# Attention in steps of four key tiles instead of two, in a two-layer convolution and attention kernel

## The chip, the cores and the metric

The kernel runs on one core of a Trainium2 chip. The metric is the device time of one execution in microseconds, taken as the median of several runs. TensorE (PE) does the matrix products, VectorE (DVE) and ScalarE (ACT) empty its results from PSUM and do the elementwise work, GpSimd (POOL) does further elementwise work, and SyncE (SP) issues the loads and stores. All data are 32-bit floats; a 512-column product in that type is two instructions on TensorE.

## The reference

The input x has 8 images of 512 channels, 32 x 32 positions each. Two layers follow one another, each added to its own input.

```python
# layer 0
t = cbs(gn(x), cv1_w)                  # 1x1, 512 -> 512; cbs = convolution, batch norm, SiLU
ys = [t[:, :256], t[:, 256:]]
for i in range(2):
    z = cbs(ys[-1], m_cv1_w[i], pad=1)  # 3x3, 256 -> 256
    q, k, v = qkv(z)                    # 1x1, 256 -> 768; 4 heads of 64
    a = softmax(q^T (k + rw + rh) / 8)  # 1024 queries x 1024 keys per head
    ys.append(ys[-1] + silu(bn(m_cv2[i] @ (a v))))
x = x + cbs(concat(ys), cv2_w)          # 1x1, 1024 -> 512
# layer 1
x = x + conv1x1(gn(x), w_eff)[:, perm]  # w_eff masked and scaled by tables made from S and T
```

gn is a group norm over 32 groups without weights; batch norm uses fixed statistics.

## The kernel before

**Units.** The 8 images with 2 attention blocks each are 16 *slots* (`slots`, two images in turn, block 0 of both, then block 1 of both). A slot is four *units*: a pair of heads (hp) times a half of the 512 queries. A unit has eight key tiles (`KT`) of 128 keys; a tile's logits are 128 keys x 2 heads x 512 queries and take two PSUM banks. `units` holds all 64 in order.

**A unit's life** (class `Unit`). `logits(t)` forms a tile on TensorE (`lg`, L510), copies it to a tile `st` on ScalarE (L517), and from tile 1 on takes the running maximum over keys on VectorE (`mx`, L522). `top` (L530, L531) transposes the maximum and reduces it; `spread` (L539) broadcasts its negative into PSUM (`mb`). `soften(t)` (L544, VectorE) adds `mb` to the tile, `exponent(t)` (L548, ScalarE) takes the exponential in place, and POOL adds the tile to the running sum in four quarters (L555). `values(t)` (L562, TensorE) multiplies by v into one bank, `po`. `finish` (L576, L579) sums the running sum over the keys with a product by ones (`den`) and copies it to `rb`; `divide` (L583, L585, VectorE) takes the reciprocal of one half of the queries and multiplies `po` by it into q.

**The order.** The main loop runs unit u's softmax and values, and next to them the logits of the following unit `nxt`. It does so in steps of two key tiles: the last two tiles' values of the unit `before`, or two tiles' values of u, then two tiles' logits of `nxt`. Between them `advance(share)` emits *filler*, the other layers' products, from `slot_filler`: the first convolution (`conv1`, L248), the 3x3 convolution of the next slot (`conv3`, six products in a row transform, L313), the query, key and value projections (`project`), `conv_m2`, `conv2` and the last layer (`last`), most of them through `accumulate` (L175). The slot is cut into 4 x 10 nominal steps, and filler is emitted up to a given share of the slot's total at steps 0.7, 1.4, 2, 4, 6, 8 and 10 of each unit. Chains of order-only dependencies (`in_turn` for VectorE, `act_turn` for ScalarE, `pe_turn` for TensorE) fix the order of the attention's instructions among themselves, and of some of the transform's, on each engine. `Clock` issues some filler work (norms, transforms) when its estimated due time is reached.

**Buffers.** PSUM has eight banks: five in turn (`ps_f`) for logits, filler, `mt` and `den`; two for `mb`; one for `po`. In SBUF the pool `stp` holds 10 tiles of logits (4 KB a partition), `wp` four weight tiles, `wt` three temporaries of the convolution's transform, `kvp` three tiles each of keys (tag k) and values. Small parameters (`bn_sb`, `s_sb`, `rw_sb`, `rh_sb`, L86 to L89, and `tri`, L681) have their own places. The parameters are used while the kernel starts, last by `positions(1)`, which adds `rw` and `rh` on POOL. All loads and stores after the start go through `load` (L77, L78) on SP's queue, in order.

**The end.** After the last unit `finish`, the last two tiles' values and `divide` follow, then filler that was held back: `conv_m2`, `conv2` and `last` of the last image.

Of the kernel before, what the change touches and what calls it, by code (L numbers as in the profile page):

```python
# [15 lines left out]
F32 = mybir.dt.float32  # L16
AF = mybir.ActivationFunctionType
ALU = mybir.AluOpType
# [4 lines left out]
P = 128  # L23
NB = 8
CT = 4
IT = 2
F = 32
HW = F * F
HALF = 512
NBLK = 2  # L30
HD = 64
NG = 16
KT = 8
NGR = 17

BN_CV1, BN_CV2, BN_M1, BN_M2, BN_ALL = 0, 4, 8, 12, 16
# [3 lines left out]
def conv_preact_kernel(ctx: ExitStack, tc: tile.TileContext, x, cv1, cv2, mcv1, qkv, mcv2, bn, rw, rh, conv, s_in, t_in, out):  # L40
    nc = tc.nc
    stt = nc.vector.scalar_tensor_tensor

    def pool(name, bufs, **kw):
        return ctx.enter_context(tc.tile_pool(name=name, bufs=bufs, **kw))

    const = pool("const", 1)
    dram = pool("dram", 1, space=bass.MemoryType.DRAM)
    small = pool("small", 2)
    qp = pool("qp", 2)  # L50
    kp_ = pool("kvp", 3)
    stp = pool("stp", 10)
    one = pool("one", 1)
    wp = pool("wp", 4)
    gx = pool("gx", 4)
    wm = pool("wm", 1)
    gy = pool("gy", 4)
    gr = pool("gr", 2)
    tp = pool("tp", 3)
    wt = pool("wt", 3)  # L60
    ps_m = pool("ps_m", 1, space=PSUM)
    ps_o = pool("ps_o", 1, space=PSUM)
    ps_f = pool("ps_f", 5, space=PSUM)
# [1 line left out]
    def pair(p, tag, name):  # L65
        return p.tile([P, 2, HALF], F32, tag=tag, name=name)

    def bank(name):
        return ps_f.tile([P, HALF], F32, tag="bank", name=name)
# [4 lines left out]
    def flat(t):  # L74
        return t.rearrange("p a b -> p (a b)")
# [7 lines left out]
        return t  # L83


    bn_sb = const.tile([P, 4, BN_ALL], F32, name="bn_sb")  # L86
    s_sb = const.tile([P, 2, CT, NG], F32, name="s_sb")
    rw_sb = const.tile([P, NBLK, IT, F], F32, name="rw_sb")
    rh_sb = const.tile([P, NBLK, IT, F], F32, name="rh_sb")  # L89


    w_m1 = [[dram.tile([P, IT, IT, 3, P], F32, name=f"w_m1_{i}_{r}") for r in range(6)] for i in range(NBLK)]
# [89 lines left out]
    def in_turn(instruction):  # L182

        if turn:
            tc.add_manual_dep(instruction.ins, turn.pop().ins.name, IN_ORDER, reason="order of VectorE")
        turn.append(instruction)

    def act_turn(instruction):

        if act_last:  # L190
            tc.add_manual_dep(instruction.ins, act_last.pop().ins.name, IN_ORDER, reason="order of ScalarE")
        act_last.append(instruction)
# [300 lines left out]
    class Unit:  # L493
# [52 lines left out]
        def exponent(self, t):  # L546
            st = flat(self.st[t])
            act_turn(nc.scalar.activation(st, st, AF.Exp))  # L548
            if t == 1:
                self.acc = pair(one, "acc", f"sum_{self.name}")  # L550
            for j in range(4 if t else 0):

                part = slice(256 * j, 256 * j + 256)
                so_far = self.st[0] if t == 1 else self.acc
                nc.gpsimd.tensor_tensor(flat(self.acc)[:, part], flat(so_far)[:, part], st[:, part], ALU.add)  # L555
# [81 lines left out]
    def tables():  # L637

        scr = flat(pair(gr, "gr", "scr")).rearrange("p (a k g) -> p a k g", a=8, g=NG)
        gi = scr[:, 0]  # L640
        gi_i = scr[:, 7].bitcast(mybir.dt.int32)
        nc.gpsimd.iota(gi_i, pattern=[[0, 2 * CT], [1, NG]], base=-NG, channel_multiplier=0)
        nc.vector.tensor_copy(gi, gi_i)
        full = [P, 2 * CT, NG]

        sc = s_sb.rearrange("p a k g -> p (a k) g")
        cols = small.tile([P, 4, 2 * CT], F32, tag="cols", bufs=1, name="cols")
        top, rsum, gain, idx = (cols[:, j] for j in range(4))

        def wide(v):  # L650
            return v.unsqueeze(2).to_broadcast(full)

        e, oh, lower = scr[:, 1], scr[:, 2], scr[:, 3]
        nc.vector.tensor_reduce(top, sc, AX.X, ALU.max)
        nc.vector.tensor_tensor(e, sc, wide(top), ALU.subtract)
        nc.scalar.activation(e, e, AF.Exp)
        nc.vector.tensor_reduce(rsum, e, AX.X, ALU.add)
        nc.vector.reciprocal(rsum, rsum)
        nc.vector.tensor_tensor(e, e, wide(rsum), ALU.mult)
        nc.vector.tensor_reduce(gain, e, AX.X, ALU.max)  # L660

        nc.vector.tensor_tensor(oh, e, wide(gain), ALU.is_equal)
        nc.vector.tensor_tensor(oh, oh, gi, ALU.mult)
        nc.vector.tensor_reduce(idx, oh, AX.X, ALU.min)
        nc.vector.tensor_tensor(oh, gi, wide(idx), ALU.is_equal)
        nc.vector.tensor_tensor(lower, gi, wide(idx), ALU.is_gt)


        pre = scr[:, 4]
        nc.vector.tensor_reduce(pre[:, 0], lower[:, CT:].rearrange("p c g -> p g c"), AX.X, ALU.add)  # L670
        for k in range(1, CT):
            nc.vector.tensor_tensor(pre[:, k], pre[:, k - 1], oh[:, CT + k - 1], ALU.add)
        yield
        oht = pair(gr, "gr", "oht")[:NG]
        for a in range(2):
            ps = bank(f"oht_{a}")
            for k in range(CT):
                nc.tensor.transpose(ps[:NG, ts(k, P)], oh[:, CT * a + k], ident)
            nc.vector.tensor_copy(oht[:, a], ps[:NG])

        tri = small.tile([P, P], F32, tag="tri", bufs=1, name="tri")  # L681
        nc.gpsimd.affine_select(
            out=tri, in_=ones, pattern=[[1, P]], compare_op=ALU.is_gt, fill=0.0, base=0, channel_multiplier=-1
        )
        rank = small.tile([P, CT], F32, tag="rank", bufs=1, name="rank")
        ps = bank("rank").rearrange("p (k g) -> p k g", g=NG)[:, :CT]
        nc.tensor.matmul(ps, ones, pre[:, :CT], start=True, stop=False)
        nc.tensor.matmul(ps, tri, oh[:, CT:], start=False, stop=True)
        nc.vector.tensor_tensor(e[:, :CT], ps, oh[:, CT:], ALU.mult)
        nc.vector.tensor_reduce(rank, e[:, :CT], AX.X, ALU.add)  # L690
        table_results.extend((gain, oht, rank))
        yield
# [48 lines left out]
    units = [Unit(im, i, hp, half) for im, i in slots for hp in range(IT) for half in range(2)]  # L741
# [25 lines left out]
    clock = Clock()  # L767
# [216 lines left out]
    first, second = images[:2]  # L984
# [8 lines left out]
    clock.at(11.0, lambda: start_norm(second, tiles2))  # L993
    clock.at(12.0, lambda: transform_weights(0))
    ranks = tables()
    clock.at(14.0, lambda: next(ranks))
    clock.at(26.0, lambda: next(ranks))
# [26 lines left out]
    before = None  # L1024
    for s in range(len(slots)):
        needed, total, todo = slot_filler(s)
        state = {"done": 0.0}

        def filler():
            for us, g in todo:  # L1030
                start = state["done"]
                for cost in g:
                    clock.tick(cost)
                    state["done"] += cost
                    yield

                state["done"] = max(state["done"], start + us)

        fill = filler()

        def advance(share):
            goal = max(share * total, min(1.0, share / 0.74) * needed + 0.1)
            while state["done"] < goal:
                if next(fill, "end") == "end":
                    break

        steps = 4 * (KT + 2)
        for j in range(4):
            u = units[4 * s + j]
            nxt = units[4 * s + j + 1] if 4 * s + j + 1 < len(units) else None  # L1050
            base = j * (KT + 2)

            advance((base + 0.7) / steps)
            u.top()
            clock.tick(0.9)
            advance((base + 1.4) / steps)
            u.spread()
            clock.tick(0.9)
            advance((base + 2) / steps)
            for t in range(0, KT, 2):  # L1060
                if before and t == 0:
                    before.finish()
                    clock.tick(0.9)
                u.soften(t)
                u.soften(t + 1)
                if t:
                    u.exponent(t)

                lag = u if t else before
                if lag:  # L1070
                    lag.values((t - 2) % KT)
                    lag.values((t - 1) % KT)
                    clock.tick(2.0)
                if before and t == 0:
                    before.divide(0)
                    before.divide(1)
                if nxt:
                    nxt.logits(t)
                    nxt.logits(t + 1)
                    clock.tick(2.0)  # L1080

                if not t:
                    u.exponent(t)
                u.exponent(t + 1)
                advance((base + 4 + t) / steps)
            before = u
        for _ in fill:
            pass

    before.finish()  # L1090
    before.values(KT - 2)
    before.values(KT - 1)
    before.divide(0)
    before.divide(1)
    im = images[NB - 1]
# [55 lines left out]
```

## Time and profile before

| quantity | value |
|---|---|
| median of 3 runs | 3161.52 us (3156.13 to 3167.02) |
| profiled execution, own time | 3162.82 us |
| its span | 3161.1 us |
| granted TensorE clock, mean | 0.996 |
| busy: TensorE, VectorE, ScalarE, POOL | 3077.0, 2049.9, 1721.0, 1398.4 us |
| logits (L510), values (L562) on TensorE | 510.9, 497.8 us in 2048 instructions each |
| softens (L544), VectorE | 512 of 1215 ns |
| maxima (L522), VectorE | 896 of 0.68 us |
| reciprocals (L583), VectorE | 128 of 1723 ns |
| copies of logits (L517), ScalarE | 1024 of 597 ns |
| exponents (L548), ScalarE | 512 of 1068 ns |
| table loads, ScalarE | 1283 ns each |
| sums (L555), POOL | 1792 of 0.77 us |

The busy time of an engine is the time in which an instruction of its own was running; the span less the busy time is idle. In the waits an entry names the engine and the operation that waited, what it waited for, and then the time in total, the number of times and the longest. In a timeline an entry has the start, the length, the engine, the source line, the operation, output and inputs, and how many like instructions are put together; the idle time ahead of it and its releaser may stand in brackets. The profile gives busy time on TensorE with modelled ends, so that neighbouring blocks overlap a little; their starts are measured.

### The profile page before, as it was taken

How to read it: one execution, taken by the hardware profiler on the slowest of the kernel's cores; microseconds unless marked ns; L12 is line 12 of the kernel's file. 1: busy time of each engine (PE TensorE's matmuls, PEld its weight loads, DVE VectorE, ACT ScalarE, POOL GpSimd, SP SyncE). 2: the span in 40 equal slices, each digit the busy share in tenths (PEclk: the TensorE clock that was granted, in tenths of full speed). 3: DMA queues.
4: the chain of work that ended last, by engine and by line, in shares of the span. 5: the costliest groups of instructions: out<-in, count | busy, mean ns of one | idle time of the engine just before them, and what ended most of it. 6: DMA issues, size and time to landing. Idle time of an engine off the chain costs nothing.

```text
span 3161.1 us, 34185 instructions
## 1 busy us (share of the span) xinstructions
PE 3077.0 (97%) x11668; PEld 1515.3 (48%) x11668; DVE 2049.9 (65%) x2718; ACT 1721.0 (54%) x2349; POOL 1398.4 (44%) x1867
## 2 busy tenths in 40 slices
PE   7999999998999999999999999999999999999999
PEld 3645354454445454455445454454445454453333
DVE  5446577567667576667666676767666676767642
ACT  3245765855655555644656455544656455546621
POOL 2104444546444554455444454445444464444520
PEclk9999999999999999999999999999999999999999
DMA  8852352421233232424233332424233332413356
GB/s 289 292 182 74 130 180 87 153 77 63 88 116 131 79 128 71 149 84 148 84 116 130 114 127 70 153 85 136 91 110 130 120 120 70 150 64 120 120 205 217
DMA packets 142014, 399.35 MB, mean 126 GB/s; under 512 B 13072, under 2 KB 14352, under 8 KB 141840
## 3 DMA queue, kind: packets, MB, share of 16 engines
q1 hardware_dynamic: 141120, 396.94, 36.6%
q8 instruction: 92, 1.51, 0.2%
q14 instruction: 82, 0.67, 0.1%
q10 hardware_dynamic: 720, 0.23, 0.0%
HBM read 317.42 MB, written 79.69 MB: 126 GB/s over the span
## 4 chain that ended last, share of the span: by engine, by line
PE 75%; DVE 4%; ACT 4%; issue 2%; DMA 1%; POOL 1%; SPq 0%; ACTq 0%; DVEq 0%; POOLq 0%
PE cv L175 15%; PE m L313 13%; PE po L562 12%; PE lg L510 12%; PE l L175 7%; PE qk L175 6%; PE v L405 3%; PE m L175 3%; PE den L576 2%; PE mb L539 2%; PE mt L530 1%; ACT st L517 1%; DVE st L544 1%; ACT st L548 1%; DVE mx L522 1%
## 5 line engine op out<-in xcount | busy, mean ns | idle before, releaser
L555 POOL TENSOR_TENSOR sum<-sum,st 128x256 f32<-128x256 f32 x1536 | 1132.0, 771 | 552.1 <-ACT st L548 547.7
L522 DVE TENSOR_TENSOR mx<-mx,lg 128x512 f32<-128x512 f32 x768 | 477.8, 682 | 417.6 <-ACT st L517 417.4
L517 ACT COPY st<-lg 128x512 f32<-128x512 f32 x1024 | 525.0, 597 | 356.1 <-PE lg L510 331.7
L548 ACT ACTIVATE st<-st 128x1024 f32<-128x1024 f32 x512 | 539.1, 1068 | 304.1 <-DVE st L544 302.9
L544 DVE TENSOR_TENSOR st<-st,mb 128x1024 f32<-128x1024 f32 x512 | 604.4, 1215 | 60.2 <-PE mb L539 60.2
L555 POOL TENSOR_TENSOR sum<-st,st 128x256 f32<-128x256 f32 x256 | 185.1, 754 | 788.8 <-ACT st L548 788.8
L313 PE MATMUL m<-plane,w_m 128*128 128x256 f32 x2304 | 528.8, 383 | 4.9 <-ACT cv2s L130 2.7
L562 PE MATMUL po<-st,v 128*64 128x512 f32 x2048 | 497.8, 605 | 18.2 <-ACT st L548 16.2
L510 PE MATMUL lg<-q,k 64*128 64x512 f32 x2048 | 510.9, 617 | 2.9 <-ACT y L130 2.9
L313 PEld LDWEIGHTS m<-plane,w_m 128*128 128x128 f32 x2304 | 426.4, 189 | 129.5 <-issue 45.1
L175 PE MATMUL cv<-y,w_cv 128*128 128x512 f32 x1024 | 464.5, 599 | 7.9 <-ACT cv2s L130 4.6
L510 PEld LDWEIGHTS lg<-q,k 64*128 64x128 f32 x2048 | 177.3, 186 | 328.2 <-issue 267.4
L175 PEld LDWEIGHTS cv<-y,w_cv 128*128 128x128 f32 x1024 | 185.8, 190 | 248.1 <-issue 226.4
L562 PEld LDWEIGHTS po<-st,v 128*64 128x64 f32 x2048 | 128.8, 136 | 323.6 <-issue 237.3
L175 PE MATMUL cv<-x,w_cv 128*128 128x512 f32 x512 | 237.0, 610 | 10.6 <-ACT y L130 3.7
L175 PE MATMUL l<-x,w_l 128*128 128x512 f32 x512 | 236.9, 606 | 7.9 <-DVE mx L522 6.9
L175 PE MATMUL qk<-z,w_qkv 128*128 128x512 f32 x512 | 234.0, 600 | 1.4 <-DVE mx L522 1.4
L583 DVE RECIPROCAL rb<-rb 128x256 f32<-128x256 f32 x128 | 215.5, 1723 | 26.0 <-ACT rb L579 25.8
L531 DVE TENSOR_REDUCE nm<-mt 128x4 f32<-128x512 f32 x128 | 82.3, 684 | 144.7 <-PE mt L530 144.7
L579 ACT COPY rb<-den 128x512 f32<-128x512 f32 x64 | 37.3, 583 | 230.4 <-PE den L576 230.4
L175 PEld LDWEIGHTS cv<-x,w_cv 128*128 128x128 f32 x512 | 95.3, 194 | 132.0 <-issue 109.3
L175 PEld LDWEIGHTS l<-x,w_l 128*128 128x128 f32 x512 | 93.4, 191 | 130.4 <-issue 112.2
(145 smaller groups left out, 2408.8 us busy)
## 6 DMA issues: line engine op xcount, KB each, us to landing
w_m<-w_m SPq DMA_DIRECT2D x96, 768.0 KB, 4.8
w_cv<-in_cv SPq DMA_DIRECT2D x90, 512.0 KB, 3.5
y<-y SPq DMA_DIRECT2D x64, 512.0 KB, 4.8
x<-in_x SPq DMA_DIRECT2D x56, 512.0 KB, 5.2
y<-y SPq DMA_DIRECT2D x64, 256.0 KB, 3.5
k<-r SPq DMA_DIRECT2D x32, 512.0 KB, 3.6
res<-y SPq DMA_DIRECT2D x32, 512.0 KB, 4.0
xr<-in_x SPq DMA_DIRECT2D x32, 512.0 KB, 4.1
```

Of the source, the lines that this page charges most:

```text
L175: nc.tensor.matmul(ps, w, moving, start=(n == 0), stop=(n == len(terms) - 1))
L313: nc.tensor.matmul(ps[:, ts(co, 256)].rearrange("p (t x) -> p t x", x=F), w[:, co, c, dx], u[:, 9 * c : 9 * c + 8, dx : dx + F], start=(j ...
L405: nc.tensor.matmul(ps[:, ts(j, P)], z[:, c, ts(4 * j4 + j, P)], w[:, c, 512 + P * hp : 512 + P * hp + P], start=(c == 0), stop=(c == IT - 1),)
L510: nc.tensor.matmul(lg[h], self.k[r, ts(t, P)], self.q[r, self.hp, ts(self.half, HALF)], start=True, stop=True)
L517: act_turn(nc.scalar.copy(st[:, h], lg[h]))
L522: in_turn(nc.vector.tensor_tensor(self.mx[:, h], so_far[:, h], lg[h], ALU.max))
L531: nc.vector.tensor_reduce(self.nm[:, h], mt, AX.X, ALU.max, negate=True)
L544: in_turn(nc.vector.tensor_tensor(st, st, flat(self.mb), ALU.add))
L548: act_turn(nc.scalar.activation(st, st, AF.Exp))
L555: nc.gpsimd.tensor_tensor(flat(self.acc)[:, part], flat(so_far)[:, part], st[:, part], ALU.add)
L562: nc.tensor.matmul(self.po[HD * h : HD * h + HD], self.v[:, t, ts(h, HD)], self.st[t][:, h], start=(t == 0), stop=(t == KT - 1),)
L583: nc.vector.reciprocal(self.rb[:, r], self.rb[:, r])
```

## The change

The main loop takes steps of four key tiles: values of two, logits of two, values of two, logits of two, with no filler between them. The values now lag four tiles instead of two. The softens and exponents of the third and fourth tile of a step are issued after the step's logits, one soften and one exponent in turn; `divide` follows both values and both logits blocks. The filler is emitted at steps 0.5, 2, 6 and 9.3 of each unit (`top` now stands ahead of the first). The ring of logits grows from 10 to 12 tiles. To make room, the weights have three tiles instead of four, the transform's temporaries two instead of three, and the small parameters lie in one tile of the keys' ring. The last unit's running sum is made on VectorE, one addition of a whole tile each (seven), in the fixed order of that engine, instead of in 28 quarters on POOL; and four tiles' values follow its denominator at the end.

```diff
-    stp = pool("stp", 10)
+    stp = pool("stp", 12)
-    wp = pool("wp", 4)
+    wp = pool("wp", 3)
-    wt = pool("wt", 3)
+    wt = pool("wt", 2)
...
-    bn_sb = const.tile([P, 4, BN_ALL], F32, name="bn_sb")
-    s_sb = const.tile([P, 2, CT, NG], F32, name="s_sb")
-    rw_sb = const.tile([P, NBLK, IT, F], F32, name="rw_sb")
-    rh_sb = const.tile([P, NBLK, IT, F], F32, name="rh_sb")
+    par = kp_.tile([P, HW], F32, tag="k", name="par")
+    def param(first, shape):
+        return par[:, first : first + P].rearrange("p (a b c) -> p a b c", b=shape[0], c=shape[1])
+    s_sb = param(0, (CT, NG))
+    rw_sb = param(128, (IT, F))
+    rh_sb = param(256, (IT, F))
+    bn_sb = par[:, 512 : 512 + 4 * BN_ALL].rearrange("p (a b) -> p a b", b=BN_ALL)
...
             if t == 1:
                 self.acc = pair(one, "acc", f"sum_{self.name}")
+            if t and self is units[-1]:
+                so_far = self.st[0] if t == 1 else self.acc
+                in_turn(nc.vector.tensor_tensor(flat(self.acc), flat(so_far), st, ALU.add))
+                return
...
-        tri = small.tile([P, P], F32, tag="tri", bufs=1, name="tri")
+        tri = par[:, 384:512]
...
-            advance((base + 0.7) / steps)
             u.top()
             clock.tick(0.9)
-            advance((base + 1.4) / steps)
+            advance((base + 0.5) / steps)
             u.spread()
             clock.tick(0.9)
             advance((base + 2) / steps)
-            for t in range(0, KT, 2):
+            half = KT // 2
+            for t in range(0, KT, half):
...
                 lag = u if t else before
-                if lag:
-                    lag.values((t - 2) % KT)
-                    lag.values((t - 1) % KT)
-                    clock.tick(2.0)
+                for pair_ in range(0, half, 2):
+                    if lag:
+                        lag.values((t + half) % KT + pair_)
+                        lag.values((t + half) % KT + pair_ + 1)
+                        clock.tick(2.0)
+                    if nxt:
+                        nxt.logits(t + pair_)
+                        nxt.logits(t + pair_ + 1)
+                        clock.tick(2.0)
                 if before and t == 0:
                     before.divide(0)
                     before.divide(1)
-                if nxt:
-                    nxt.logits(t)
-                    nxt.logits(t + 1)
-                    clock.tick(2.0)
                 if not t:
                     u.exponent(t)
                 u.exponent(t + 1)
-                advance((base + 4 + t) / steps)
+                for key in (t + 2, t + 3):
+                    u.soften(key)
+                    u.exponent(key)
+                advance((base + (6 if not t else 9.3)) / steps)
             before = u
...
     before.finish()
-    before.values(KT - 2)
-    before.values(KT - 1)
+    for key in range(KT // 2, KT):
+        before.values(key)
```

## The prediction

> **What bounds the kernel now.** I read the page's busy shares and chain first, then the windows, the waits of TensorE, and TensorE's timeline inside one attention unit. Page, busy time and chain:
>
> ```profile
> PE 3077.0 (97%) x11668; PEld 1515.3 (48%) x11668; DVE 2049.9 (65%) x2718; ACT 1721.0 (54%) x2349; POOL 1398.4 (44%) x1867
> ...
> PE 75%; DVE 4%; ACT 4%; issue 2%; DMA 1%; POOL 1%; SPq 0%; ACTq 0%; DVEq 0%; POOLq 0%
> ```
>
> TensorE is the bound: 84.0 us of the span are not its own. The windows (length, PE, PEld, DVE, ACT, POOL, clock, DMA share, GB/s) say where those lie:
>
> ```profile
> 0.00:20.00 20.00, 2.55 (x6) 1.84 (x7) 13.15 (x43) 3.86 (x6) 8.10 (x19) 1.00 0.90 330
> ...
> 400.00:800.00 400.00, 384.70 (x1558) 195.67 (x1557) 280.23 (x367) 252.23 (x342) 194.95 (x260) 1.00 0.32 108
> 800.00:1200.00 400.00, 396.53 (x1551) 197.58 (x1549) 267.91 (x343) 227.40 (x308) 191.98 (x257) 1.00 0.32 108
> ...
> 3000.00:3050.00 50.00, 44.10 (x117) 17.61 (x116) 31.18 (x32) 21.90 (x25) 20.80 (x29) 0.93 0.47 163
> ```
>
> 17.45 us are the start, 12.7 lie behind 3000 us (5.9 of them in the last row), 2.0 between 20 and 200, and the windows from 200 to 3000 us, length less PE, sum to 51.8. What ended them:
>
> ```profile
> PE po L562 <- ACT st L548: 16.2, 14, 3.7
> ...
> PE l L175 <- DVE mx L522: 6.9, 3, 2.5
> PE gv_b L156 <- DVE gd_b L152: 5.9, 1, 5.9
> ```
>
> The largest is the values (po) waiting for the exponents. Busy time itself hides a loss. TensorE inside a unit, and a stretch of one tile shape near the end (start, length):
>
> ```profile
> 1503.68 1.99 PE L510 MATMUL lg<-q,k 64*128 64x512 f32 x8
> 1505.59 5.42 PE L175 MATMUL m<-q,w_m 128*128 128x512 f32 x12
> 1510.94 1.94 PE L562 MATMUL po<-st,v 128*64 128x512 f32 x8
> 1512.81 1.99 PE L510 MATMUL lg<-q,k 64*128 64x512 f32 x8
> 1514.73 5.45 PE L313 MATMUL m<-plane,w_m 128*128 128x256 f32 x24
> 1520.11 1.94 PE L562 MATMUL po<-st,v 128*64 128x512 f32 x8
> ...
> 3122.75 32.86 PE L175 MATMUL l<-x,w_l 128*128 128x512 f32 x76
> ```
>
> Ends are modelled, so I use starts. Unswitched, a 512-column matmul takes (32.86 - 0.59)/75 = 0.430 us. The m block runs from 1505.59 to 1510.94, 5.35 us where 12 take 5.16: 0.19 over. The convolution block takes 5.38 for 24 half-length ones (5.16): 0.22 over. The logits take 1.92 against 1.72, the values 1.87 against 1.72. So every change of tile shape costs about 0.20 us.
>
> **The change part by part.**
>
> *Order of the attention steps.* Today each two tiles are filler, V, L, filler: three changes of shape per two tiles. The new order, filler, V, L, V, L, filler, has five per four tiles. In the two built orders the filler blocks between attention groups fall from 260 to 149, and all changes of shape from 772 to 662. Work is equal. 111 x 0.20 = **-22 us**. Bounds: 110 x 0.15 = -17 (the values' price) and 111 x 0.22 = -24.
>
> *Waits of the values for exponents.* Longer filler blocks are also longer covers. In the built orders the filler between the first logits group of a unit and its first values goes from a median of 5.3 to 10.5 us of TensorE work; between the last logits and the denominator from 13.1 to 18.2. The chain to be covered before the first values is four copies (0.6 each behind the last logits, about 1.5 us sticking out), a table load (1.28) and two exponents (1.07 each): 4.9 us. Before, 5.3 just covers it, and the 14 waits result; after, nine units keep under 5.3. The chain to the denominator, copies, exponents 5 to 7 and three POOL sums of 2.8, is about 11 us, covered by 13.9 or more in most units. I take 9 of the 16.2 us away. Another 7 us I take from other waits: the convolution's wait for L522 (6.9 us) falls with x2 loads that the new order issues with 65.6 us of TensorE work ahead instead of 9.1. Sum **-16 us**; bounds 0 (waits move) and -51.8 (all from 200 to 3000 us). What is late next is the evacuation of banks.
>
> *New waits for PSUM banks.* This speaks against the change. The second logits pair takes four banks of five, while the first pair's four are being emptied, with only one values block (1.87 us) between where there were 5.4 of filler. Its third bank of reuse, tile 1's first half, is wanted 1.87 + 0.96 = 2.83 us after the first pair ended. One bad and one good evacuation today, rows from the timeline:
>
> ```profile
> 1504.91 2.05 ACT L517 COPY st<-lg 128x512 f32<-128x512 f32 x4 [2.23 <-PE lg L510]
> ...
> 1505.13 3.36 DVE L583 RECIPROCAL rb<-rb 128x256 f32<-128x256 f32 x2
> ...
> 1509.01 1.28 DVE L522 TENSOR_TENSOR mx<-st,lg 128x512 f32<-128x512 f32 x2
> ...
> 1523.83 2.48 DVE L522 TENSOR_TENSOR mx<-mx,lg 128x512 f32<-128x512 f32 x4 [1.90 <-ACT st L517]
> ```
>
> In the bad one the maximum stands behind two reciprocals; its first half ends at 1509.69, 4.02 us after the logits: 4.02 - 2.83 = 1.2 us late. In the good one the first bank is free 2.5 us after its first tile began, in time. Over the 64 units the first half of tile 1 is free a median 2.3 us after the logits (worst tenth from 4.0), the one of tile 5 1.75 us (worst quarter from 2.7). In the new order the reciprocals still stand ahead of the first maxima (both in 52 units, one in 10), but first logits follow mb by 6.3 instead of 4.1 us of TensorE work, so softens and reciprocals start earlier against them. Bounds: 0, and 1.2 in each of 128 groups, 154 us. I take it in ten groups, about today's worst tenth: **+12 us**. The four POOL sums per tile hold the twelve tiles longer, but the second pair's copies go into tiles whose sums end 3 us earlier at the median cover: 0; today copies wait 24.2 us for sums, off the path.
>
> TensorEngine Tiling (Array Packing) in the Trainium skill, section PSUM Bottleneck, speaks against this edit: packing "speeds up TensorE but not PSUM evacuation". The row beside it: a first group of 7.6 us on TensorE asks VectorE for two softens 2.4, two reciprocals 3.4, six maxima 4.1 and two products 0.7, 10.6 us. If that decided in every unit, 64 x 3 us would be added and the sum would be 3162.8 - 38 + 192 = 3317; by the rows it does not, since softens and reciprocals run beside the filler and the denominator ahead of the group.
>
> *Exponents and tables.* 34 fewer table loads (224 to 190) of 1.28 us leave ACT 44 us; ACT is 54% busy and off the path: 0 here, the gain is the cover above. ScalarE: Activation LUTs in the Trainium skill, section What ACT_TABLE_LOAD costs, has 2.66 us per switch with its drain; the trace shows 1.28 us and the next instruction 0.02 us behind it (1506.98, 1508.28), so the row is taken; by the page ACT would gain 90 us, still off the path.
>
> *Last unit's sums on VectorE.* 28 POOL sums of 0.77 (21.6 us) go; seven full-width sums of 1.2 (the soften's row) come, 8.5 us on VectorE. Tail before, each engine's timeline:
>
> ```profile
> 3009.41 16.46 POOL L555 TENSOR_TENSOR sum<-sum,st 128x256 f32<-128x256 f32 x24 [1.20 <-ACT st L548]
> ...
> 3016.98 8.90 DVE L150 TENSOR_TENSOR gd_b<-mv_b,gms_b 128x4 f32<-128x4 f32 x1
> ...
> 3026.33 0.59 PE L156 MATMUL gv_b<-gd_b,gmat 128*128 128x4 f32 x2 [5.90 <-DVE gd_b L152]
> ```
>
> A four-column VectorE operation lasts until POOL's sums end (3025.87), and gv_b waits 5.9 for it. That goes. But den now waits for VectorE: eight softens 9.7, seven sums 8.5, reciprocals and products 4.1, the filler's operations some 6, between them exponents it waits for: about 37 us after mb (2996.5), against 30 us of TensorE work up to den (36 less the 5.9). Wait about 6 to 7 instead of 5.9: **0**, bounds -6 and +7. Behind den stand four values and then conv_m2.
>
> *Three weight buffers, two temporaries, small parameters in a key tile.* TensorE work between a weight buffer's release and the next load's first use falls from at least 18.2 to 12.0 to 13.7 us, in two cases 6.9 and 10.3; loads land in 4.8 us (768 KB) and 3.5 (512 KB). Hidden by those covers: **0**; the bound is 10 us, if SP, whose loads go in order, holds two behind a late release. Three y tiles lead by 5.1 instead of 9.1 us: at most +1.5, in those 10. The temporaries are read on VectorE, in order: 0. The parameters' tile is free once POOL has added the positions, by 144 us, before 200 us: 0, bounds -2 (all idle time of 20 to 200 us) and +3 (two POOL operations there, 2.67).
>
> Sum against the profiled execution, 3162.8 (span 3161.1): -22 - 16 + 12 = -26, so **3137 us**. That execution is 1.3 above the median 3161.5, nothing beside the unknowns.
>
> **The rivals.**
> - *Shapes pay, the old waits only move* and new ones take 12: 3162.8 - 22 + 12 = 3153. For: the exponents' chain is as long as before. Against: the doubled filler.
> - *Deep cut:* two thirds of the 51.8 go (34) and new waits cost 2: 3109. For: few units are left under their cover. Against: many small waits have other causes.
> - *Eaten:* new bank waits of about 35 us, 0.27 per group: 3160, no change.
> - *Slower:* evacuation becomes the bound. Place: the second logits pair behind maxima that stand behind reciprocals and the filler's VectorE work. It decides once new waits exceed 22 + 16 + 9.5 = 47.5 us, 0.37 us per group of 128; at 1.2 us in three of four groups it is +115: 3240. For: five banks, and VectorE's 10.6 us. Against: the median 2.3 us lies under 2.83.
>
> **How the numbers follow.** A measurement tells about 0.3%, 9.5 us, from no change. Chances: forecast (3125 to 3148) 0.42, deep cut 0.17, waits only move 0.12, eaten 0.12, slower 0.17. Faster 0.42 + 0.17 + 0.12 = 0.71, same 0.12, slower 0.17. Range: the low end leaves out the deepest half of the deep cut, 3108; the high end leaves out the slower case past its beginning, 3172. About 0.2 lie outside.
>
> **What would show it.** Right: TensorE busy near 3055; logits starting 1.9 us behind values, values behind logits; the wait of po for L548 under 8 us; a new group, lg waiting for ACT or DVE (L517, L522), near 12. Wrong: that group above 40; the den wait far over 7; w_m or w_cv waits from DMA of more than a few us; a busy time that didn't fall although shapes change less, which would mean that a change between the two small shapes costs more than one with the filler.

## The result: slower, and where the time came from

The changed kernel takes 3206.01 us (median of 6 runs, 3202.23 to 3208.28) against 3157.14 us of the kernel before on the same chips: a ratio of 1.0145, interval 1.0132 to 1.0157. Forecast were 3137 us and a range from 3108 to 3172.

The page of the changed kernel, busy time and chain:

```profile
PE 3096.0 (97%) x11668; PEld 1548.6 (48%) x11668; DVE 2065.2 (65%) x2725; ACT 1690.2 (53%) x2315; POOL 1379.6 (43%) x1839
...
PE 71%; DVE 7%; ACT 5%; issue 5%; DMA 4%; POOL 2%; SPq 0%; DVEq 0%; ACTq 0%; POOLq 0%
```

TensorE's share is still 97%, though the span is 39 us longer: busy time grew by 19 us and idle time by 20. The count of matmuls is the same, so some of that busy time is waiting inside blocks, or slow matmuls. The chain says it better: VectorE from 4 to 7%, DMA from 1 to 4%, issue from 2 to 5%.

The windows that changed most at the ends (length, PE, PEld, DVE, ACT, POOL, clock, DMA share, GB/s), first in the kernel before, then in the changed one:

```profile
150.00:200.00 50.00, 48.45 (x173) 24.58 (x171) 16.15 (x30) 21.16 (x33) 1.02 (x1) 1.00 0.52 182
...
3050.00:3100.00 50.00, 48.55 (x112) 20.58 (x111) 9.73 (x15) 3.91 (x6) 0.00 (x0) 1.00 0.70 241
```

```profile
150.00:200.00 50.00, 40.60 (x145) 21.45 (x144) 6.11 (x14) 16.73 (x27) 1.02 (x1) 0.90 0.42 143
...
3050.00:3100.00 50.00, 38.29 (x90) 15.44 (x91) 14.26 (x21) 9.17 (x12) 1.02 (x1) 0.88 0.53 171
```

In both windows of the changed kernel TensorE is idle for some 10 us and its granted clock falls to 0.90 and 0.88. (The changed kernel is some 20 us later in its work by 3000 us, so the second pair of windows doesn't hold quite the same work.) TensorE's waits, two of the kernel before and then those of the changed one:

```profile
PE mb L539 <- DVE nm L531: 0.7, 2, 0.3
...
PE den L576 <- POOL sum L555: 0.3, 1, 0.3
```

```profile
PE lg L517 <- DVE mx L529: 14.8, 8, 4.7
...
PE mb L546 <- DVE nm L538: 9.5, 7, 2.7
PE m L320 <- DVE mx L529: 8.8, 6, 2.0
PE qk L182 <- DMA w_qkv<-in_qkv: 7.4, 1, 7.4
PE den L588 <- POOL sum L567: 7.3, 8, 4.1
PE cv L182 <- DMA y<-y: 7.3, 3, 6.0
...
PE den L588 <- DVE sum L561: 5.9, 1, 5.9
...
PE po L574 <- ACT st L555: 2.3, 1, 2.3
```

The wait of the values for exponents fell from 16.2 to 2.3 us. In its place stand logits waiting for maxima (14.8; none such before), mb and den waiting (9.5 and 7.3, before 0.7 and 0.3), and one long wait each at the start (qk) and at the end (y).

**A ledger.** The starts of the matmul records allow a fuller account than the waits. Each stretch of one tile shape lasts to the start of the next. Off it I take its matmuls at the unswitched rate (0.430 us for two of the half-shape instructions of logits, values and den, or for one of 512 columns in the full shape) and the price of entering and leaving the shape (0.197 us for logits, 0.155 for values and den, 0.199 for filler, the undisturbed blocks' own excess). What is left is stall, slow matmuls after a wait included. In the profiled executions, in us ("units" is from the first unit's mb to the last unit's; the first 14 us of the start are left out):

| | shapes | stall: start | units | end |
|---|---|---|---|---|
| before | 142.0 | 10.2 | 67.0 | 16.6 |
| changed | 120.1 | 22.5 | 107.3 | 25.7 |
| difference | -21.9 | +12.3 | +40.3 | +9.1 |

The sum is +39.8, the spans differ by 39.4. The column of shapes is the number of blocks times the price of an undisturbed one; the changed kernel's undisturbed blocks have the forecast price, and so the column falls by the forecast 22 us. Three other places took that nearly three times over (61.7 us).

The stalls in the units by place (us); "second pair" is the step's second block of logits with the values ahead of it, and includes the filler between the two pairs, where there is any. In the old order there is always some; in the changed one the built order has some in a few units.

| | second pair, first step | second pair, second step | mb to den | den and values |
|---|---|---|---|---|
| before | 15.5 | 14.7 | 10.9 | 0.7 |
| old order, new buffers (an experiment) | 16.6 | 12.2 | 15.4 | 0.8 |
| changed | 10.2 | 45.6 | 29.1 | 8.4 |

### The profile page after: what moved, and what is told of

It reads as the page before. It is cut to its first block, busy times and chain, and to the rows that moved or that the text cites. A ratio compares the mean times of both kernels' runs of the same rounds, so it can differ in the third digit from the quotient of the medians.

```text
span 3200.5 us, 34160 instructions
## 1 busy us (share of the span) xinstructions
PE 3096.0 (97%) x11668; PEld 1548.6 (48%) x11668; DVE 2065.2 (65%) x2725; ACT 1690.2 (53%) x2315; POOL 1379.6 (43%) x1839
## 4 chain that ended last, share of the span: by engine, by line
PE 71%; DVE 7%; ACT 5%; issue 5%; DMA 4%; POOL 2%; SPq 0%; DVEq 0%; ACTq 0%; POOLq 0%
PE cv L182 14%; PE m L320 12%; PE lg L517 12%; PE po L574 12%; PE qk L182 6%; PE l L182 5%; PE v L412 3%; DVE st L551 2%; POOL sum L567 2%; PE den L588 2%; PE mb L546 2%; ACT st L555 1%; PE m L182 1%; PE mt L537 1%; ACT st L524 1%
## 5 line engine op out<-in xcount | busy, mean ns | idle before, releaser
L567 POOL TENSOR_TENSOR sum<-sum,st 128x256 f32<-128x256 f32 x1512 | 1118.9, 777 | 332.9 <-ACT st L555 332.7
L555 ACT ACTIVATE st<-st 128x1024 f32<-128x1024 f32 x512 | 527.7, 1058 | 168.3 <-DVE st L551 161.9
L517 PE MATMUL lg<-q,k 64*128 64x512 f32 x2048 | 541.7, 622 | 16.4 <-DVE mx L529 14.8
L320 PE MATMUL m<-plane,w_m 128*128 128x256 f32 x2304 | 521.7, 382 | 15.8 <-DVE mx L529 8.8
L517 PEld LDWEIGHTS lg<-q,k 64*128 64x128 f32 x2048 | 193.0, 187 | 357.0 <-issue 196.6
L182 PEld LDWEIGHTS qk<-z,w_qkv 128*128 128x128 f32 x512 | 95.7, 192 | 126.1 <-issue 111.4
```

Of the source, the lines that this page charges most:

```text
L182: nc.tensor.matmul(ps, w, moving, start=(n == 0), stop=(n == len(terms) - 1))
L320: nc.tensor.matmul(ps[:, ts(co, 256)].rearrange("p (t x) -> p t x", x=F), w[:, co, c, dx], u[:, 9 * c : 9 * c + 8, dx : dx + F], start=(j ...
L517: nc.tensor.matmul(lg[h], self.k[r, ts(t, P)], self.q[r, self.hp, ts(self.half, HALF)], start=True, stop=True)
```

## The experiments

Each was compared with the kernel before on the same chip.

**Buffers alone.** `w3_only`: before, with

```diff
-    wp = pool("wp", 4)
+    wp = pool("wp", 3)
```

> The kernel before with three weight tiles instead of four, nothing else changed. Theory L (late loads): the first projection's weights come some 8 to 10 us late at the start and the last image's loads stand behind weight loads on SP's queue at the end, as in the changed kernel, 3157 + 12 + 9 = 3178 us, and some of the waits inside the units appear too, up to 3195. Theory B (banks): the start and the end belong to the new order or to the parameters' tile, and this kernel takes 3155 to 3162 us.

`old_order`: the changed kernel's buffers (12 logits tiles, 3 weight tiles, 2 temporaries, the parameters' tile) with the old loop and POOL's sums.

> The old order of the attention steps, and POOL's sums for the last unit, with every buffer of the changed kernel: twelve logits tiles, three weight tiles, two temporaries, the parameters in a key tile. Theory B: stalls of TensorE between the first and the last unit's mb stay near 67 us, as before, and only the start and the end lose, 3165 to 3180 us. Theory L: most of the 40 us of new stalls inside the units show here as well, 3195 us or more.

Measured: 3171.87 us (1.0043, 1.0029 to 1.0057) and 3172.44 us (1.0038, 1.0026 to 1.0050), against 3159.14. The third weight tile alone costs 13 us, and the other buffers add nothing to it. The ledger puts it at the start (stall 21.8 and 21.0 us, before 10.2); the units keep 68.8 and 69.5, and the end is no worse than before (10.4, 11.7). TensorE's wait in `w3_only`:

```profile
PE qk L175 <- DMA w_qkv<-in_qkv: 7.5, 1, 7.5
```

So theory L (late loads) holds for the start and falls for the units and the end. The units' stalls belong to the new order, the end's to it or to the last unit's sums on VectorE, which `old_order` leaves on POOL too.

**The fourth weight tile given back.** `split_weights`: two tiles for the large weights, two for the small ones.

```diff
-    wp = pool("wp", 3)
+    wp = pool("wp", 2)
-        t = wp.tile([P, *shape], F32, tag="w", name=name)
+        t = wp.tile([P, *shape], F32, tag="wb" if shape in ((IT, 768), (IT, IT, 3, P)) else "ws", name=name)
```

> The changed kernel with two tiles for the large weights (convolution products, projections) and two for the small ones, four in all. Theory L: the first projection's weights are no longer behind another load and the end's store is not held, 10 to 25 us less, 3180 to 3196 us. Theory B for the units, and if the end is held by something else: 3200 to 3208 us. If two tiles for the products are too few, w_m waits appear on TensorE and it is slower, above 3215 us.

Measured: 3195.81 us (1.0110, 1.0082 to 1.0139). The start's stall falls from 22.5 to 9.9 us, the wait for w_qkv is gone; units (103.8) and end (29.6) stay. It confirms the start and nothing else.

**The last unit's sums.** `last_pool`: the changed kernel without the branch for `units[-1]`.

> The changed kernel with the last unit's sums on POOL again. If the sums on VectorE cost nothing, as predicted, the same within 3 us, 3203 to 3209 us. If the wait of the denominator for VectorE (5.9 us and the slow matmuls after it) is their cost, 3198 us; if POOL's sums would have ended later than VectorE's, 3210 to 3215 us.

Measured: 3201.01 us (3192.79 to 3207.67; 1.0123, 1.0094 to 1.0152). The interval overlaps the changed kernel's; the end's stall is 18.4 instead of 25.7 us. At most a few us, not settled.

**What holds the banks?** In the changed kernel's trace one place repeats in three of the four image pairs. TensorE's timeline, then VectorE's:

```profile
1321.90 1.99 PE L517 MATMUL lg<-q,k 64*128 64x512 f32 x8
1323.82 1.94 PE L574 MATMUL po<-st,v 128*64 128x512 f32 x8
1325.69 3.70 PE L182 MATMUL cv<-y,w_cv 128*128 128x512 f32 x8
1333.38 4.11 PE L517 MATMUL lg<-q,k 64*128 64x512 f32 x8 [3.99 <-DVE mx L529]
```

```profile
1327.77 1.29 DVE L437 TENSOR_TENSOR ybuf<-res,m2s 128x512 f32<-128x512 f32 x2 [7.65 <-DMA res<-y]
...
1332.64 1.88 DVE L529 TENSOR_TENSOR mx<-mx,lg 128x512 f32<-128x512 f32 x3
```

The first logits pair is done at 1323.8. Its maxima come at 1332.6, because in VectorE's order conv_m2's residual addition stands ahead of them and waits 7.65 us for its load; behind it come two softens and work of the transform, some 3.8 us, before the maxima. The second pair waits for banks until 1333.4, and its matmuls then take 4.11 instead of 1.99 us. Counted over all places where logits waited, or were waited for, about half, 36 of 75 us by my count, lay where residual additions stood ahead of the maxima (an expectation below says 36 of 58, a miscount). The three places of this kind hold some 20 of the 45.6 us at the second step's second pair; the rest lies in many units, mostly at 1 to 2.5 us each. The runs that follow go after this and the two other suspects, ScalarE's exponents and the reciprocals.

`no_res`: the load left out, the addition kept (of the result to itself, so that the blocks' residual is missing).

```diff
-                load(res, y_dram[n][1 + i][:, :, ts(h, HALF)])
...
-                    nc.vector.tensor_tensor(dst, res[:, co], t, ALU.add)
+                    nc.vector.tensor_tensor(dst, t, t, ALU.add)
```

> The changed kernel without the residual of the blocks: conv_m2's result is added to itself instead of to the loaded residual, so that VectorE's work is the same and the 32 loads are left out. If VectorE waiting for these loads (42 us of its idle time) ahead of the maxima is what holds the banks, 25 to 35 us of the stalls inside the units go, 3175 us. If not, 3200 us, only what the lighter SP queue gives.

Measured: 3178.24 us (1.0063, 1.0047 to 1.0080), 28 us less than the changed kernel. The units' stall falls from 107.3 to 85.7 us, the end's from 25.7 to 20.1. The late loads are a cause, though the edit also takes 32 loads off the queue (`gr3_t2` below keeps them). They are not the whole: by the same account the second pair of the second step still stalls some 34 us, against 45.6 with the loads and 12.2 in the old order.

`res_early`: both residual loads ahead of the first half's stores in program order.

```diff
-            for h in range(2):
-                res = pair(gr, "gr", f"res_{name}_{h}")
-                load(res, y_dram[n][1 + i][:, :, ts(h, HALF)])
+            both = [pair(gr, "gr", f"res_{name}_{h}") for h in range(2)]
+            for h in range(2):
+                load(both[h], y_dram[n][1 + i][:, :, ts(h, HALF)])
+            for h in range(2):
+                res = both[h]
```

> The changed kernel with both residual loads of conv_m2 ahead of the first half's stores on SP's queue. In the changed kernel some 36 of the 58 us that logits wait for banks lie where residual additions stand ahead of the maxima on VectorE. If the second residual, held on SP behind stores that wait for VectorE, is what makes VectorE late, 15 to 25 us of the stalls inside the units go (107 to about 87) and the time is near 3185 us. If the additions themselves or ScalarE's work decide, not the load, 3200 to 3208 us.

Measured: 3210.84 us (1.0162, 1.0144 to 1.0180): no gain. The trace says why. Relative to conv_m2's first product (1310 us in the changed kernel) the second residual was issued after 11.9 us and landed after 18.1; with `res_early` after 11.0 and 17.7. The stores were not what held it. It follows a weight load in SP's queue:

```profile
SPq L78 <- PE m L182: 15.1, 1, 15.1
```

This is SP's wait between 1296 and 1325 us of the changed kernel, for conv_m2's own matmuls to free a weight tile; the second residual needs a tile of a ring of two besides.

`gr3`, and `gr3_t2`, which takes the room from the half tiles instead of the x ring:

```diff
-    gr = pool("gr", 2)
+    gr = pool("gr", 3)
# gr3
-    gx = pool("gx", 4)
+    gx = pool("gx", 3)
-    tiles = start(first, gx, "gx")
+    tiles = start(first, stp, "st")
# gr3_t2
-    tp = pool("tp", 3)
+    tp = pool("tp", 2)
```

> The changed kernel with three residual tiles instead of two, so that both of conv_m2's loads stand ahead of the weight load for the convolution on SP's queue (room is made with three instead of four x tiles; the first image starts in logits tiles). In the changed kernel SP waits 15 us for conv_m2's own weights to come free, with the second residual behind that weight load. Theory Q (that queue holds the residual, the residual VectorE, VectorE the banks): 25 us less, as without the residual (3178): 3178 to 3185 us. If the load is late for another reason, or three x tiles cost as much, 3200 us or more.

> The changed kernel with three residual tiles, the room taken from the half tiles (two instead of three) and not from the x ring, which in the last runs cost 21 us in the old order (three waits of some 10 us for an image's statistics). Theory Q: VectorE's waits for residuals fall from 42 to under 5 us and 20 to 25 us of the stalls inside the units go, as without the residual: 3180 to 3187 us. If two half tiles hold ScalarE's results back, or the residual was not the cause, 3200 us or more.

`w4`: four weight tiles, with the same three x tiles as `gr3`. `before_gr3`: the edit of `gr3` in the kernel before.

> The changed kernel with four weight tiles (same room). Theory Q: the weight load ahead of the residual finds a free tile and waits less, so that the residual comes earlier, about half of the 25 us; and the first projection's weights are in time, 10 to 12 us: 3206 - 12 - 12 = 3182 us. If the fourth tile serves only the start: 3195 us.

> The kernel before with three residual tiles and three x tiles. In its trace VectorE waits 15 us for residuals, against 42 in the changed one, with filler between the logits pairs. By theory Q little of that reaches TensorE: 3152 to 3160 us. If the three x tiles cost something, it shows here: above 3165 us.

Measured: `gr3` 3218.00 us (1.0185), `w4` 3251.83 us (1.0288), `before_gr3` 3180.00 us (1.0063, 1.0044 to 1.0082). The x ring was a bad place to take room: the control loses 21 us, mostly to three waits of this kind (its waits of TensorE):

```profile
PE gm_a L146 <- DVE mv_a L144: 23.1, 3, 13.7
```

`gr3_t2` has no such wait: 3192.70 us (1.0108, 1.0089 to 1.0128), 13 us under the changed kernel. VectorE's waits for residuals, first in the changed kernel, then in `gr3_t2`:

```profile
DVE ybuf L437 <- DMA res<-y: 24.5, 4, 8.4
...
DVE res L437 <- DMA res<-y: 17.5, 4, 6.9
```

```profile
DVE res L437 <- DMA res<-y: 2.7, 1, 2.7
```

42.0 us become 2.7; logits waiting for maxima fall from 14.8 to 5.6 us, while logits waiting for conv_m2's SiLU rise from 1.1 to 7.3, which may be the price of two half tiles. In `w4` 39.0 us of residual waits remain: a free weight tile does not bring the loads earlier, a third residual tile does. That part of theory Q (the queue) falls; the ring of two is what decides when the loads come. Why `w4` takes 34 us more than `gr3` stays open. With its loads in time `gr3_t2` too keeps some 34 us at the second step's second pair.

Why the loads are late only in the new order can be read from the traces, and no run isolates it. In the slots of this place (block 0), the products of conv_m2 start within 10.5 us in `old_order`, spread over two blocks of filler, and the second residual lands 15 to 18 us after the first of them. In the changed kernel the longer block holds them all, in 6.5 us, and the residual lands after 15 to 19.

`exp_late`: exponent 4 behind the step's logits. `div_late`: divide behind the maxima, in VectorE's fixed order.

```diff
# exp_late
-                if t:
-                    u.exponent(t)
...
-                if not t:
-                    u.exponent(t)
+                u.exponent(t)
                 u.exponent(t + 1)
# div_late: the two calls of divide go from ahead of these lines to behind them
                 for key in (t + 2, t + 3):
                     u.soften(key)
                     u.exponent(key)
+                if before and t == 0:
+                    before.divide(0)
+                    before.divide(1)
...
-            nc.vector.reciprocal(self.rb[:, r], self.rb[:, r])
+            in_turn(nc.vector.reciprocal(self.rb[:, r], self.rb[:, r]))
```

> The changed kernel with the exponent of tile 4 behind the step's logits instead of ahead of them in ScalarE's order. If that exponent with its table load holds the copies of the first logits pair, the three places per image pair that it precedes (about 3 us each time round) go, some 10 us, 3196 us. If VectorE alone decides, 3203 to 3209 us; if POOL's sums then end too late for the denominator, 3215 us or more.

> The changed kernel with the reciprocals and products of divide in VectorE's fixed order, behind the maxima and the softens of the step. If reciprocals ahead of maxima hold the banks, as the prediction had it, about 10 us go, in four to six places with two reciprocals of 1.7 us each: 3196 us. If they seldom stand in the way, 3203 to 3209 us; later values waiting for po would make it slower, above 3212 us.

Measured: 3219.61 us (1.0191, 1.0174 to 1.0208) and 3258.06 us (1.0311, 1.0284 to 1.0337). Both make a new wait on the other side. First `exp_late`, where the sums end too late for den (7.3 us before the edit), then `div_late`, where the next values wait for po:

```profile
PE den L588 <- POOL sum L567: 18.7, 10, 5.2
```

```profile
PE po L574 <- DVE q L597: 35.1, 15, 8.6
```

`all_three` (with `res_early` and `split_weights`):

> The three together, and two tiles each for large and small weights. If the bank waits are the sum of these three causes and the start returns with the fourth weight tile (measured alone: 10 us less), 3206 - 20 - 10 - 10 - 10 = 3156 us, level with the kernel before. If the causes replace one another, 3175 us or more.

3264.57 us (1.0336): it inherits both waits.

`exp_spread`: softens and exponents of tiles 2 and 3 in the middle of the filler.

```diff
+                if not t:
+                    advance((base + 4) / steps)
                 for key in (t + 2, t + 3):
```

> The changed kernel with the softens and exponents of tiles 2 and 3 in the middle of the filler that follows the first step, instead of behind exponents 0 and 1 at once; TensorE's order is kept. If four exponents in a row hold ScalarE's work for the filler, and through it VectorE and the banks at the second step, 10 to 25 us less, 3180 to 3196 us. If not, 3200 to 3210 us; more if the values then wait for these exponents.

Measured: 3207.81 us (1.0154, 1.0132 to 1.0177), as the changed kernel. Four exponents in a row, as the changed kernel has them there, are not the cause.

**Which step?** `first_grouped` keeps four tiles together in the first step only, `second_grouped` in the second only; in the other step filler and exponents stand between the pairs. In `second_grouped` the filler takes over the reciprocal's half tile before divide has read it, so that its quotients are not the attention's; its instructions are the same.

```diff
                 for pair_ in range(0, half, 2):
+                    if pair_ and t != 0:              # second_grouped: t != 4
+                        ...
+                        u.exponent(t + 1)
+                        u.soften(t + 2)
+                        u.exponent(t + 2)
+                        advance((base + (4 if not t else 7.3)) / steps)
...
-                advance((base + (6 if not t else 9.3)) / steps)
+                advance((base + (5 if not t else 9.3)) / steps)   # second_grouped: 6, 9.3
```

> The changed kernel with four tiles together only in a unit's first step; in the second, filler (and exponents) between the two pairs as before. Split by place, the stalls of the changed kernel lie at the second pair of the second step (46 us with the filler slipped in ahead of it, against 12 in the old order), between mb and the denominator (29 against 15) and behind the denominator (8 against 1), while the second pair of the first step has no more than the old order. Theory S (second step): some 50 us of new stalls go, 11 us of the shape gain go too: 3206 - 50 + 11 = 3167 us, at best 3155. Theory A (any four tiles together): the stalls move to the first step or stay, 3190 us or more.

> The converse: filler between the pairs of the first step, four tiles together in the second. Theory S: the stalls stay, half of the shape gain goes, 3206 + 11 = 3217 us, not under 3205. Theory A: half of the stalls go, 3190 us.

Measured: 3195.49 us (1.0114, 1.0099 to 1.0130) and 3209.96 us (1.0153, 1.0130 to 1.0176). By place theory S is right: the second pair of the second step has 22.1 us with filler between the pairs (`first_grouped`), 45.6 in the changed kernel, and at least 45 in `second_grouped`. But `first_grouped` got 10.5 us back, not 40. Its shape changes cost 12.0 us more than the changed kernel's, and of the stalls only 8.6 us in the units and 15.1 at the end are gone. Its last logits stand closer to the transposes, and the stretch from mb to den rises from 29.1 to 50.1 us, the transposes (mt) being the largest wait there:

```profile
PE mt L537 <- DVE mx L529: 28.1, 10, 4.9
```

Two attempts at a faster kernel went further. `first_split` adds the split weights and POOL's sums, `fg_gr3` has the buffers of `gr3` and filler points at 4.6, 6.6 and 9.3.

> Four tiles together in the first step only, two tiles each for large and small weights, the last unit's sums on POOL. If the parts add, 10 us for the start and 5 for the end below the kernel with the first step grouped: 3152 us by theory S, faster than the kernel before (3159); by theory A 3175 us or more.

> Three residual tiles, and four tiles together only in the first step, with the filler points at 4.6, 6.6 and 9.3 so that the last logits pair has as much filler before the transposes as in the kernel before (with 5, 7.3, 9.3 these waited 28 us for maxima). From 3195: 20 us less by the points, 15 less by the residuals, 3160 us, level with the kernel before. If the maxima stay late, 3180 us.

3197.69 us (1.0122, 1.0106 to 1.0138) and 3271.43 us (1.0353). In `first_split` the start gains (stall 13.0) and the end loses it again (20.3 instead of 10.6). In `fg_gr3` the transposes wait 11.1 us, but shorter filler ahead of the values stalls the second step's first pair (27.3 us), on top of the x ring's cost. No version beat the kernel before.

## Why the prediction was wrong

- *Shapes*, -22: right in the number of blocks and in the price of an undisturbed one; the ledger has -21.9. TensorE's busy time rose all the same, from 3077 to 3096 us. The prediction would have read that as a dear change between the two small shapes. It is not that (1.92 and 1.94 us, last section): it is slow matmuls after waits.
- *Waits for exponents and other old waits*, -16: the waits named did go (po for L548 16.2 to 2.3, l for L522 6.9 to 0.8). But the same step called the cover of the denominator sufficient; den's wait for POOL's sums rose from 0.3 to 7.3 us.
- *New waits for banks*, +12: this is the step that failed. It had the mechanism, five banks and a late maximum, at the wrong place and a wrong size. I priced it at the first step, behind reciprocals, in ten groups at 1.2 us, and took nothing for the second step. There the stalls went from 12.2 to 45.6 us. In the first step they went from 16.6 in the old order to 10.2, but the 16.6 counts the filler ahead of the pair, so that a few us more at the pair itself, as foretold, are not excluded. Of the 33 us in the second step some 11 go without the residual loads; over the whole kernel 28 us go without them, and 13 with a third residual tile. What holds the other 22 us at that pair was not isolated. I had taken the lag of maxima behind logits from the trace of before as if it belonged to the maxima. It belongs to what stands ahead of them on VectorE, and the longer filler blocks change that.
- The sign I had named for this, logits waiting near 12 us, came out (14.8), and would have passed for a success: the list of waits leaves out the slow matmuls behind a wait and the filler that waits in the logits' stead, and the ledger counts both.
- The rival *Slower* (0.17) had the right resource and, of its two causes, one that the runs show, the filler's work on VectorE. The other, reciprocals, no run shows: moving them behind the maxima made the kernel slower.
- TensorEngine Tiling (Array Packing) in the Trainium skill, section PSUM Bottleneck, which I weighed there, says that tiling speeds up TensorE and not the emptying of PSUM. In kind this case agrees: waits for banks took the gain. Its size doesn't follow from VectorE's total work: the 192 us that I worked out so are far from the 40.3 us by which the units' stalls grew.
- *Last unit's sums*, 0: the terms were right (gv_b's wait is gone, den waits 5.9 us for VectorE where 6 to 7 were expected), the sum was not. The four values behind den ran slowly, and later conv2 waited 6.0 us for y loads; the end's stall rose by 9.1 us. `last_pool` suggests, and does not settle, that the sums are part of it.
- *Three weight buffers*, 0 with a bound of 10: +13, all at the start (`w3_only`, `split_weights`). I had counted TensorE's work between release and use inside the units, and not in the first 200 us, where the wait for w_qkv appeared (7.4 us).

Still open: about 16 us of the units' stalls (85.7 in `no_res` against 69.5 in `old_order`). They lie at the second step's second pair (some 34 us there against 12.2) and between mb and den. The end's 9 us are settled no better. Moving an exponent or the reciprocals there only moved the wait.

## What to carry to other kernels

When two blocks of interleaved work are merged, the work between them is merged too: read the filler's own chain (loads, additions, stores) at its new density, and not only the covers that grow. A lag read from a trace belongs to the queue that it was read in; ask what will stand ahead of the instruction in the new order. Price a buffer taken away at every place where it is used, the start too: here the whole cost lay there.

## What the runs showed of the hardware

A change between the two small shapes costs as much as one with the full array. TensorE's timeline of the changed kernel, one undisturbed first step:

```profile
1521.51 1.89 PE L574 MATMUL po<-st,v 128*64 128x512 f32 x8
1523.33 1.99 PE L517 MATMUL lg<-q,k 64*128 64x512 f32 x8
1525.25 1.94 PE L574 MATMUL po<-st,v 128*64 128x512 f32 x8
1527.12 2.02 PE L517 MATMUL lg<-q,k 64*128 64x512 f32 x8
1529.06 3.21 PE L182 MATMUL m<-q,w_m 128*128 128x512 f32 x6
```

From start to start the logits take 1.92 us ahead of values and 1.94 ahead of filler. So in this kernel only fewer blocks save time, whatever their neighbours.

The matmuls behind a wait of some 6 us are slow too. Sixteen instructions of values in the changed kernel's last unit, undisturbed and behind den's wait:

```profile
3023.93 3.60 PE L574 MATMUL po<-st,v 128*64 128x512 f32 x16
...
3055.11 1.97 PE L588 MATMUL den<-sum,ones 128*64 128x512 f32 x4 [5.86 <-DVE sum L561]
3056.87 5.57 PE L574 MATMUL po<-st,v 128*64 128x512 f32 x16
```

3.60 us become 5.57, and den's four take 1.97 instead of the 1.08 of an undisturbed den, so the 5.9 us wait was followed by nearly 3 us of loss; the granted clock of the window from 3050 to 3100 us was 0.88.
